# Query, key and value projections from seven products of quarters, with the biases in a weight row, in a graph attention and transformer kernel

## The chip, the cores and the metric

The kernel runs on one core of one Trainium2 chip. The metric is the device time of one execution in microseconds (us); lower is better. All inputs and outputs are float32, the adjacency int32.

## The reference

For 64 graphs of 256 nodes with 256 features, two layers follow each other. Layer 0 is two graph attentions, a residual with layer norm, and a feed-forward of 1024 with ReLU, again with residual and layer norm. Layer 1, where the change lies, is attention of 8 heads of 32, in which the values depend on the relation (0 to 3) that the adjacency gives, and a feed-forward of 1024 with GELU:

```python
q = (src @ Wq + bq).reshape(Bb, Nn, h, dh).transpose(0, 2, 1, 3)
k = (src @ Wk + bk).reshape(Bb, Nn, h, dh).transpose(0, 2, 1, 3)
scores = jnp.einsum('bhid,bhjd->bhij', q, k) / np.sqrt(dh)
attn = jax.nn.softmax(scores, axis=-1)
for r in range(Wv.shape[0]):
    v_r = (src @ Wv[r] + bv[r]).reshape(Bb, Nn, h, dh).transpose(0, 2, 1, 3)
    mask = (adj_matrix == r)[:, None]
    out = out + jnp.einsum('bhij,bhjd->bhid', attn * mask, v_r)
attn_out = out.transpose(0, 2, 1, 3).reshape(Bb, Nn, Dm) @ Wo + bo
x = _ln(src + attn_out, g1, beta1)
ff = jax.nn.gelu(x @ W1 + b1, approximate=False) @ W2 + b2
return _ln(x + ff, g2, beta2)
```

The adjacency that comes in holds only 0 and 1, so two of the four relations can occur.

## The kernel before, in words

Two paths are built. `narrow_path` computes everything under assumptions (adjacency of 0 and 1, sums of exponentials in range) and sums up checks of them; only where a check fails does `general_path` run after it. `checked` (L704) is the check of the adjacency: VectorE forms (a - 1) a and sums it per partition into a column of `other`; the sums are compared with 0 at L1448.

The graphs are taken in 32 groups of two. A group has T = 4 blocks of 128 nodes, 512 nodes in all. Features lie on partitions where they are contracted: `hT` holds 256 features as KB = 2 tiles of 128 partitions by 512 nodes. Group u goes through layer 0 one turn before it goes through layer 1, and its first graph attention one turn before that: `turn(y_, x_, z)` (L1155) works on three groups at once, y in layer 1, x in layer 0's feed-forward and z in the graph attentions. In turns 0 to 29 all three are there; turn 30 lacks z, turn 31 lacks x and z. On TensorE, SyncE, VectorE and ScalarE the order of instructions in these turns is the order of the Python code, up to small exchanges (`tc.manual_schedule`); in the last turn only TensorE and SyncE keep it.

The names that matter:

- `projection` (L979): q and k. Each is two output halves of 128 features; a half is two matmuls of 128x128 weights by 512 nodes into one bank of PSUM (L986), then a ScalarE activation adds the bias column and writes SBUF (L988).
- `values` (L992): for each of the 4 node blocks, two matmuls with 128 nodes as stationary operand and the 512 columns of `wv` (relation 0, and relation 1 minus relation 0) as moving one (L999); VectorE adds the bias row `rbv` (L1001).
- `weighted` (L1006): the scores of one graph and four heads (a "quad"), eight matmuls (L1015), and four exponentials on ScalarE (L1021). `masked` (L1024) multiplies by the adjacency (L1026), `node_sums` (L1029) adds over node blocks (L1031), `applied` (L1034) forms the products with the values (L1041) and the sums of the exponentials (L1044, tile `zo`), and `divided` (L1047) divides (L1052 to L1057). `add_blocks` (L780) then multiplies by `wo` (L786).
- `hidden_seven` (L842) and `HiddenOut` (L930): both feed-forwards already come from seven products of quarters. The quarters are halves of the features by the two graphs. VectorE makes four differences (L854), TensorE does seven products per half of the outputs (L871) into two banks, ScalarE copies one bank out (L880), VectorE adds the other to it (L883). Those banks are used again by later products, which therefore wait for the copy or the sum. In the second factor, VectorE makes the sums `eq` and `eaq` (L946), TensorE the products (L960), VectorE adds them to `y` (L968).
- `norm` (L805) computes means and variances on VectorE (L801, L802) and the reciprocal root on GpSimd (L812, L813); `applied_norm` (L818) makes `nm` on VectorE (L821) and applies it in four ScalarE activations (L828). `times` and `plus` (L836, L839) put the affine part on the residual, on VectorE.
- `normed_features` (L663) turns normed rows into features: VectorE transposes 32x32 blocks (L668), then 16 moves put them in place, 4 by GpSimd copies and 12 by SyncE transfers of 32 KB (L677, L687). With `natural` set, the result has nodes in order; this is the `hT` of layer 1.
- `folding` (L603) folds the layer norms' scale and shift into the next weights at the start, spread over the start of the program by `next(fold)`: `shifted` (matmuls with one column, L592), `scaled` on GpSimd (L599), `seven` and `seven_out` (the weight sums for the seven products, on GpSimd).
- The tiles of `work` are named by tags, two buffers each unless `bufs=1`; `bank` gives one of six banks of PSUM, and `po` and `zo` have one each.

The first lines of a turn are

```python
query(0)
query(1)
if X:
    applied_norm(X["y"], *X.pop("n"))
last = norm(waiting[0][0], 3, waiting[0][1]) if waiting else None
key(0)
key(1)
if X:
    X["hT"] = normed_features(x_, 0, X["y"])
    times(X["y"], rg1)
scores(0)
```

Of the kernel before, what the change touches and what calls it, by code (L numbers as in the profile page):

```python
# [9 lines left out]
F32 = mybir.dt.float32  # L10
# [6 lines left out]
P = 128  # L17
# [368 lines left out]
def narrow_path(  # L386
# [123 lines left out]
    def gat_weights():  # L510
# [5 lines left out]
        a1, a2 = columns([v.rearrange("f o -> (f o)") for v in (g_a1, g_a2)], "ga", nc.scalar, "k")  # L516
# [31 lines left out]
    lg1, lb1, bf1, lg2, lb2, bq, bk, lg3, lb3, b1 = columns(  # L548
        (g_g1, g_b1, g_bf1, g_g2, g_b2, t_bq, t_bk, t_g1, t_be1, t_b1), "cols", nc.scalar, "q")
    rg1, rb1, rg2, rb2 = row(g_g1, "rg1"), row(g_b1, "rb1"), row(g_g2, "rg2"), row(g_b2, "rb2")  # L550

    wq, wk, wo = weight(t_Wq, "wq"), weight(t_Wk, "wk"), weight(t_Wo, "wo")
# [4 lines left out]
    rbv = row(t_bv[0:2].rearrange("r f -> (r f)"), "rbv")  # L557
    nc.vector.tensor_tensor(wv[:, :, 1, :], wv[:, :, 1, :], wv[:, :, 0, :], ALU.subtract)
    nc.vector.tensor_tensor(rbv[:, F:], rbv[:, F:], rbv[:, :F], ALU.subtract)
# [3 lines left out]
    def seven(w, name):  # L563


        h = FF // 2
# [34 lines left out]
    wf1s, wf2s, w1s, w2s = [], [], [], []  # L601

    def folding():  # L603
# [8 lines left out]
        for w, bias, name in ((wq, bq, "bq"), (wk, bk, "bk")):  # L612
            shifted(w, range(KB), lb2, bias, name)
            scaled(w, lg2)
        yield
        ps = bank("rbvp")
        for k in range(KB):
            nc.tensor.matmul(ps, lb2[:, k:k + 1].to_broadcast([P, P]), wv[:, k].rearrange("p r f -> p (r f)"),
                             start=(k == 0), stop=(k == KB - 1))
        nc.vector.tensor_tensor(rbv, rbv, ps, ALU.add)  # L620
        scaled(wv.rearrange("p c r f -> p c (r f)"), lg2)
# [12 lines left out]
    for n, (rb, v) in enumerate(((rb1, g_bf2), (rb2, t_bo), (rb3, t_b2))):  # L634
        nc.gpsimd.tensor_add(rb, rb, row(v, None, rows[:, n, :F]))

# [25 lines left out]

    def normed_features(u, l, xn, natural=False, queues=(nc.sync,)):  # L663
# [7 lines left out]
        if natural:  # L671
            hT = work.tile([P, KB, TN], F32, tag="hT", name=f"hT{u}_{l}")
            to = hT.rearrange("c k (t a r) -> c (k t) a r", a=Q, r=32)
            for q in range(Q):
# [3 lines left out]
            return [hT[:, k] for k in range(KB)]  # L678
# [25 lines left out]
    def checked(u, aq):  # L704
        a = aq.rearrange("p t n -> p (t n)")
        nc.vector.scalar_tensor_tensor(a, a, 1.0, a, op0=ALU.subtract, op1=ALU.mult,
                                       accum_out=other[:, u:u + 1])
# [20 lines left out]
    class Softmax:  # L728

        def __init__(s, u, l, wh, rows, c):  # L730
            s.u, s.wh, s.rows, s.c = u, wh, rows, c
            s.s = (work.tile([P, T, N], F32, tag="s", name=f"s{u}_{l}", bufs=1) if u > 1 else
# [246 lines left out]
    def projection(u, hT, name, w, c):  # L979

        d = work.tile([P, KB, TN], F32, tag=name, name=f"{name}{u}", bufs=1)

        def step(m):
# [509 lines left out]
```

## Time and profile before

| | |
|---|---|
| median of 3 runs | 3075.3 us (3073.74, 3075.30, 3075.54) |
| span of the profiled execution, first to last instruction | 3072.8 us |
| what lies around the span, against the median | 2.5 us |
| mean granted TensorE clock | 0.995 |
| busy: TensorE, VectorE, ScalarE, GpSimd | 3031.3, 2595.7, 1602.2, 648.0 us |
| q and k products (L986, 512 records), values (L999, 512 records) | 232 and 228.5 us of TensorE |
| one full turn | 93.4 us |

The profile has no device time of its own for the profiled execution beside its span, so the median of the runs stands for it. A float32 matmul appears as two records; a few are missing from the trace, as can be seen from their counts. Times in the profile are in microseconds from the first instruction. In the chain of waits each line is a start, a length and the engine, tile and line that held the end up; in a timeline a line is a start, the busy time, the engine, the line, the operation with its tiles and shapes, and in brackets the idle time before it with what ended it.

### The profile page before, as it was taken

Reading aid. Unit: us, or ns where it says so; the run is one execution under the profiler, and the core shown is the slowest. Engines: PE = TensorE matmul, PEld = TensorE weight load, DVE = VectorE, ACT = ScalarE, POOL = GpSimd, SP = SyncE. Lnnn points to the kernel's source line nnn. Section 1 sums busy time; section 2 is a strip of 40 time slices with the busy share of each in tenths; the row PEclk is TensorE's granted clock in tenths of the full one; section 3 lists DMA queues with packets and bytes.
Section 4 is the critical chain, followed back from the end, with each engine's and each line's share of the span. In section 5 each row is a group of like instructions: output and inputs, shape, how many; then the busy total and the mean of one; then the engine's idle time right before and its main releaser. Section 6 shows DMA issues by size and latency. Waiting matters only on the chain.

```text
span 3072.8 us, 56424 instructions
## 1 busy us (share of the span) xinstructions
PE 3031.3 (99%) x21432; PEld 2330.1 (76%) x21432; DVE 2595.7 (84%) x4890; ACT 1602.2 (52%) x3212; POOL 648.0 (21%) x896
## 2 busy tenths in 40 slices
PE   7999999999999999999999999999999999999998
PEld 6677877778777778777787777787777787777866
DVE  4788888888888888888888888888888888888876
ACT  4455545555545555555555455555455554554553
POOL 3122121222211221212221112222112212122211
PEclk8999999999999999999999999999999999999999
DMA  5011111211111211112211112111112111121000
GB/s 149 13 37 35 34 39 25 44 41 35 35 35 32 44 37 32 39 26 43 44 33 35 40 25 44 37 36 35 30 38 44 35 34 39 25 44 37 18 13 16
DMA packets 427988, 113.37 MB, mean 37 GB/s; under 512 B 364568, under 2 KB 427072, under 8 KB 427712
## 3 DMA queue, kind: packets, MB, share of 16 engines
q1 hardware_dynamic: 417664, 102.46, 15.8%
q10 hardware_dynamic: 8992, 6.19, 0.8%
q8 instruction: 172, 2.82, 0.4%
q0 software_dynamic: 1056, 1.05, 0.1%
q14 instruction: 104, 0.85, 0.1%
HBM read 57.04 MB, written 16.78 MB: 24 GB/s over the span
## 4 chain that ended last, share of the span: by engine, by line
PE 90%; DVE 7%; DMA 1%; POOL 1%; ACT 1%; issue 0%; SPq 0%; ACTq 0%; POOLq 0%; DVEq 0%
PE yf L960 22%; PE h1a L871 15%; PE h1b L871 11%; PE po L1041 8%; PE vp L999 7%; PE sp L1015 4%; PE xpp L715 4%; PE yop L786 4%; PE qp L986 3%; PE kp L986 3%; PE ygp L786 3%; PE zo L1044 2%; PE hpp L775 2%; DVE s L750 2%; DVE yt L668 1%; DVE eaq L946 1%
## 5 line engine op out<-in xcount | busy, mean ns | idle before, releaser
L880 ACT COPY h<-h1b 128x512 f32<-128x512 f32 x384 | 224.6, 585 | 390.0 <-PE h1b L871 390.0
L828 ACT ACTIVATE y<-y,nm,rs 128x256 f32<-128x256 f32 x450 | 239.0, 591 | 238.4 <-DVE nm L821 234.1
L883 DVE TENSOR_TENSOR h<-h1a,h 128x512 f32<-128x512 f32 x384 | 263.6, 687 | 117.5 <-PE h1a L871 111.6
L1026 DVE TENSOR_TENSOR ea<-e,aT 128x1024 f32<-128x1024 f32 x256 | 309.5, 1239 | 54.3 <-ACT e L1021 54.3
L1021 ACT ACTIVATE e<-sp 128x512 f32<-128x512 f32 x512 | 264.3, 602 | 52.0 <-PE sp L1015 48.7
L1054 POOL TENSOR_TENSOR low<-low,rq 128x16 f32<-128x16 f32 x64 | 13.9, 218 | 1087.3 <-DVE rq L1053 1087.3
L685 POOL COPY hT<-yt 32x256 f32<-32x256 f32 x244 | 207.2, 849 | 59.0 <-DVE yt L668 51.4
L968 DVE TENSOR_TENSOR y<-yf,y 128x256 f32<-128x256 f32 x448 | 183.1, 409 | 39.7 <-PE yf L960 39.6
L999 PE MATMUL vp<-wv,hT 128*128 128x512 f32 x480 | 214.0, 599 | 0.0
L801 DVE BATCH_NORM_STATS2 st<-y 128x6 f32<-128x256 f32 x512 | 207.7, 408 | 5.5
L812 POOL TENSOR_SCALAR rs<-mv 128x4 f32<-128x4 f32 (+1 forms) x134 | 34.2, 255 | 720.7 <-DVE mv L802 454.6
L999 PEld LDWEIGHTS vp<-wv,hT 128*128 128x128 f32 x480 | 88.7, 190 | 110.4 <-issue 103.2
L840 DVE TENSOR_TENSOR y<-y,rb 128x1024 f32<-128x1024 f32 (+1 forms) x130 | 166.9, 1284 | 3.2
L988 ACT ACTIVATE q<-qp,cols 128x512 f32<-128x512 f32 x64 | 44.0, 687 | 238.3 <-PE qp L986 238.3
L914 ACT ACTIVATE h<-h,cols 128x512 f32<-128x512 f32 x256 | 167.0, 714 | 1.5 <-DVE h L883 1.1
L837 DVE TENSOR_TENSOR y<-y,rg 128x1024 f32<-128x1024 f32 (+1 forms) x130 | 161.8, 1245 | 2.2 <-ACT y L828 1.1
L1031 DVE TENSOR_TENSOR es<-e 128x1024 f32<-128x1024 f32 x128 | 155.5, 1215 | 0.0
L677 POOL COPY hT<-yt 32x256 f32<-32x256 f32 x120 | 115.6, 964 | 169.2 <-DVE yt L668 159.7
L1015 PEld LDWEIGHTS sp<-q,k 32*128 32x128 f32 x2048 | 92.5, 184 | 74.2 <-issue 44.8
L1015 PE MATMUL sp<-q,k 32*128 32x256 f32 x2048 | 146.6, 400 | 2.0 <-ACT k L988 2.0
L1041 PE MATMUL po<-e,v 128*32 128x256 f32 x2048 | 136.3, 384 | 0.0
L813 POOL TENSOR_TENSOR rs<-rs,mhalf 128x4 f32<-128x4 f32 (+1 forms) x134 | 134.5, 1004 | 8.2
(249 smaller groups left out, 7191.4 us busy)
## 6 DMA issues: line engine op xcount, KB each, us to landing
hT<-yt SPq DMA_DIRECT2D x912, 32.0 KB, 2.0
y<-in_x_dram SPq DMA_DIRECT2D x32, 512.0 KB, 4.7
xq<-in_x_dram SPq DMA_DIRECT2D x240, 64.0 KB, 2.2
aq<-in_adj_dram SPq DMA_DIRECT2D x240, 64.0 KB, 2.4
out_dram<-y SPq DMA_DIRECT2D x30, 512.0 KB, 2.9
hT<-yt ACTq DMA_DIRECT2D x180, 32.0 KB, 1.9
wf<-in_L_gnn_w_ff_dram SPq DMA_DIRECT2D x2, 1024.0 KB, 8.1
w<-in_L_gnn_W_dram SPq DMA_DIRECT2D x2, 1024.0 KB
```

Source lines behind the costliest of these rows:

```text
L786: nc.tensor.matmul(ps[:, i * F:(i + 1) * F], lhs(t, k), rhs(b, k), start=(k == 0), stop=(k == n - 1))
L801: nc.vector.bn_stats(st[:, t, :], y[:, t, :])
L828: mark["normed"] = nc.scalar.activation(y[:, t, :], y[:, t, :], AF.Identity, bias=nm[:, t:t + 1], scale=rs[:, t:t + 1])
L871: nc.tensor.matmul(ps[:, i * N:(i + 1) * N], w_[:, f * P:(f + 1) * P], m, start=first and i == 0, stop=True, skip_group_check=True)
L880: mark["copied"] = nc.scalar.copy(out(h, o, b), pair(ps))
L883: mark["added"] = nc.vector.tensor_tensor(out(h, o, b), pair(one[h]), out(h, o, b), ALU.add)
L960: nc.tensor.matmul(s.ps[n][:, i * F2:(i + 1) * F2], a[:, k, i * P:(i + 1) * P], w_[:, k, :], start=n in (1, 2, 5) and i == 0 and k == 0, s ...
L999: nc.tensor.matmul(ps, hT[k][:, t * P:(t + 1) * P], wvf[:, k, :], start=(k == 0), stop=(k == KB - 1))
L1015: nc.tensor.matmul(ps[a][:, j * N:(j + 1) * N], k_[hp, m, j0:j0 + P], q[hp, m, b * N:(b + 1) * N], start=True, stop=True)
L1021: mark[f"exp{b * KB + m}"] = nc.scalar.activation(e[:, a, :], ps[a], AF.Exp, scale=isd)
L1026: nc.vector.tensor_tensor(ea[:, a:a + 2, :], e[:, a:a + 2, :], ab[:, None, :].to_broadcast([P, 2, NB * N]), ALU.mult)
L1041: nc.tensor.matmul(po[hp, m * N:(m + 1) * N], vs[:, hp], w[:, a, j * N:(j + 1) * N], start=(n == 0), stop=(n == len(terms) - 1))
```

## The change

1. The weights of q and k are laid into one tile `wqk` (256 by 512; each half of the columns holds 128 outputs of q and then the same 128 of k), and each of `wqk` and `wv` gets the weight sums of the seven products through `seven`. A class `Projections` takes the place of `projection` and `values`: four differences on VectorE into a tile of tag `e` (`sums`), then seven products for q and k together and seven for the values, two matmuls of 256 columns each. Products 2, 5 and 3 go through one bank, 1, 6, 7 and 4 through another; for the values these are the banks `zo` and `po`. ScalarE copies four results out of each pair of banks, VectorE adds three.
2. The biases go into a weight row. A normed row sums to zero, so feature 224 is minus the sum of the others: `joined` subtracts its weights from all rows and puts the bias in its row, and `with_ones` writes ones over that feature in `hT` (a GpSimd memset of one partition). The scalings of q, k and v weights move from GpSimd to VectorE, and the shifts of all three are matmuls of 512 columns.
3. In the turn, products of q and v alternate, the scores of the first quad stand among them, with their exponentials and masks in two parts; the norm of x is applied in two parts; the second quad's scores follow all the products. `times` on x's residual moves from before the first scores to just before `plus`.
4. `checked` is a ScalarE activation (a - 0.5) squared, summed, and compared with 0.25 for each entry; in a turn it stands after the second graph attention's exponentials, and the loads of the next adjacency follow it there.
5. Tags: the graph attention's scores of groups 2 and up share `v`, `rz` goes to `es`, and `qk` holds what `q` and `k` held.

```diff
+    def joined(w, name, bias):
+        ps, pr = bank(f"{name}bp"), bank(f"{name}rp")
+        for k in range(KB):
+            nc.tensor.matmul(ps, lb2[:, k:k + 1].to_broadcast([P, P]), w[:, k],
+                             start=(k == 0), stop=(k == KB - 1))
+        only = work.tile([P, 1], F32, tag="ve", name=f"{name}o")
+        nc.vector.tensor_mul(only, ident[:, one], lg2[:, KB - 1:KB])
+        nc.tensor.matmul(pr, only.to_broadcast([P, P]), w[:, KB - 1], start=True, stop=True)
+        nc.vector.tensor_tensor(bias, bias, ps[one].rearrange("p (o f) -> p o f", o=2), ALU.add)
+        for k in range(KB):
+            nc.vector.scalar_tensor_tensor(w[:, k], w[:, k], lg2[:, k:k + 1], pr,
+                                           op0=ALU.mult, op1=ALU.subtract)
+        nc.vector.tensor_copy(w[one, KB - 1].rearrange("p (o f) -> p o f", o=2), bias)
...
-        for w, bias, name in ((wq, bq, "bq"), (wk, bk, "bk")):
-            shifted(w, range(KB), lb2, bias, name)
-            scaled(w, lg2)
+        joined(wqk, "wqk", brow[:, 0:2])
+        wqks.extend(seven(wqk, "wqk"))
         yield
...
-        scaled(wv.rearrange("p c r f -> p c (r f)"), lg2)
+        joined(wvf, "wv", brow[:, 2:4])
+        wvs.extend(seven(wvf, "wv"))
...
+    def with_ones(hT):
+        nc.gpsimd.memset(hT[KB - 1][one], 1.0)
+        return hT
...
-            for q in range(Q):
+            for q in reversed(range(Q)):
...
-            return [hT[:, k] for k in range(KB)]
+            return with_ones([hT[:, k] for k in range(KB)])
...
     def checked(u, aq):
         a = aq.rearrange("p t n -> p (t n)")
-        nc.vector.scalar_tensor_tensor(a, a, 1.0, a, op0=ALU.subtract, op1=ALU.mult,
-                                       accum_out=other[:, u:u + 1])
+        nc.scalar.activation(a, a, AF.Square, bias=mhalf[:, 0:1], accum_out=other[:, u:u + 1])
...
+        def step(s, x, n):
+            a11, a12, a22, s1, s2, s3, s4 = wqks if x == "q" else wvs
+            w, m = {1: (a11, s.h[0][0]), 2: (a12, s.h[1][0]), 5: (s1, s.t[0]), 3: (s4, s.h[1][1]),
+                    6: (s2, s.t[1]), 7: (s3, s.t[2]), 4: (a22, s.t[3])}[n]
+            if n == 1:
+                s.one[x] = s.bank(x, 1)
+            elif n == 2:
+                s.two[x] = s.bank(x, 0)
+            ps = (s.two if n in (2, 5, 3) else s.one)[x]
+            for i in range(2):
+                l, r = (w[:, i * P:(i + 1) * P], m) if x == "q" else (m[:, i * P:(i + 1) * P], w)
+                nc.tensor.matmul(ps[:, i * N:(i + 1) * N], l, r, start=n in (1, 2, 5) and i == 0, stop=True,
+                                 skip_group_check=True)
+            if n == 2:
+                s.copied(x, 0, 0, ps)
+                s.added(x, 0, 0)
+            elif n == 5:
+                s.copied(x, 1, 1, ps)
+            elif n == 3:
+                s.copied(x, 0, 1, ps)
+            elif n == 6:
+                s.added(x, 0, 1)
+            elif n == 7:
+                s.added(x, 1, 1)
+            elif n == 4:
+                s.copied(x, 1, 0, ps)
...
         with order:
-            query(0)
-            query(1)
+            p.sums()
+            p("q1 v1 q2")
             if X:
-                applied_norm(X["y"], *X.pop("n"))
+                applied_norm(X["y"], *X["n"], [0, 1])
             last = norm(waiting[0][0], 3, waiting[0][1]) if waiting else None
-            key(0)
-            key(1)
+            p("v2 q5")
             if X:
+                applied_norm(X["y"], *X.pop("n"), [2, 3])
                 X["hT"] = normed_features(x_, 0, X["y"])
-                times(X["y"], rg1)
-            scores(0)
+            scores(0, ())
+            p("v5")
+            powers(0, (0, 1))
...
+            p("q3 v3")
+            masks(0, (0,))
+            powers(0, (2, 3))
             if waiting:
                 applied_norm(waiting[0][1], *last)
-            if X:
-                v = values(y_, hT, range(T // 2, T), v)
+            p("q6 v6 q7 v7")
+            masks(0, (2,))
+            totals(0)
+            p("q4 v4")
...
             first("4a 7b rb")
             if X:
+                times(X["y"], rg1)
                 plus(X["y"], rb1)
...
             Z["m"].exp(1)
+            checked(z, Z["aq"])
+            if z + 1 < NG:
+                load_adjacency(z + 1)
...
-            checked(z, Z["aq"])
-            if z + 1 < NG:
-                load_adjacency(z + 1)
...
-    nc.vector.tensor_scalar(good[:, 1:2], c[:, 3:4], 0.0, None, op0=ALU.is_le)
+    nc.vector.tensor_scalar(good[:, 1:2], c[:, 3:4], 0.25 * NG * T * N, None, op0=ALU.is_le)
```

## The prediction

> **What bounds the kernel now.** I read the shares of the engines first, then the chain of waits for the whole span and for one turn of the loop over groups, then the timelines of VectorE and ScalarE in that turn, last SyncE's queue.
>
> ```profile
> PE 3031.3 (99%) x21432; PEld 2330.1 (76%) x21432; DVE 2595.7 (84%) x4890; ACT 1602.2 (52%) x3212; POOL 648.0 (21%) x896
> ...
> PE 90%; DVE 7%; DMA 1%; POOL 1%; ACT 1%; issue 0%; SPq 0%; ACTq 0%; POOLq 0%; DVEq 0%
> ```
>
> TensorE is never out of work, and 90% of the chain is its own. VectorE, at 84%, is close behind. The chain in order of time (start, length, what), one turn's first stage and a piece of its hidden layer:
>
> ```profile
> 1604.16 3.44 PE qp L986 x8
> 1607.60 3.43 PE kp L986 x8
> 1611.03 1.08 PE sp L1015 x16
> 1612.11 7.06 PE vp L999 x16
> 1619.17 1.08 PE sp L1015 x16
> 1620.25 1.86 PE po L1041 x32
> ...
> 1631.57 0.86 PE h1a L871 x4
> 1632.43 0.94 PE h1b L871 x4
> ```
>
> The stage runs from 1604.16 to 1620.25: **16.09 us**, of which q, k and values take 3.44 + 3.43 + 7.06 = **13.93**, without a gap. The next turn's qp begins at 1697.60, so a turn is 93.4 us. L871 is already a product of seven: two 128x128 by 256 matmuls, each two records, in 0.86 us.
>
> Timelines of the same turn (start, busy, engine, line; in brackets the idle time before and what ended it), ScalarE, then VectorE:
>
> ```profile
> 1608.22 2.06 ACT L828 ACTIVATE y<-y,nm,rs 128x256 f32<-128x256 f32 x4
> ...
> 1633.41 0.59 ACT L880 COPY h<-h1b 128x512 f32<-128x512 f32 x1 [1.22 <-PE h1b L871]
> ```
> ```profile
> 1606.84 0.16 DVE L821 SCALAR_TENSOR_TENSOR nm<-mv,rs 128x4 f32<-128x4 f32 x1 [1.24 <-POOL rs L813]
> ...
> 1609.36 1.43 DVE L668 STREAM_TRANSPOSE yt<-y 128x256 f32<-128x256 f32 x4 [0.22 <-ACT y L828]
> ...
> 1628.85 0.72 DVE L1052 STREAM_TRANSPOSE rz<-zo 128x512 f32<-128x512 f32 x1 [2.36 <-PE zo L1044]
> ...
> 1636.15 0.69 DVE L883 TENSOR_TENSOR h<-h1a,h 128x512 f32<-128x512 f32 x1 [0.77 <-PE h1a L871]
> ```
>
> VectorE waits little: 2.36 us at L1052 and 0.77 at L883 are its two reserves in the first half of a turn. And the twelve moves of the next group's features, whose landing VectorE (L854) and TensorE wait for (two turns):
>
> ```profile
> 1797.79 7.54 SPq L687 DMA_DIRECT2D hT<-yt  x12
> ```
> ```profile
> 2732.92 8.58 SPq L687 DMA_DIRECT2D hT<-yt  x12
> ```
>
> **What the Trainium skill says.** "TensorE: Matmul & The Clock Gate", section "Back-to-back issue gap": the spacing of a stream of matmuls goes with their columns, and weight loads run beside them. The trace agrees in proportion: 512 columns take 3.44/8 = 0.43 us a record, 256 columns 0.86/4 = 0.215; halving costs nothing. "PSUM — Partial Sum Buffer", section "PSUM bank collisions raise a hardware error": accesses of different engines to a bank must be kept apart by waits. So a product written into a bank waits for the copy out of it, as L871 does here (0.94 in place of 0.86). The same page, "Engine vs sequencer instructions": ScalarE and VectorE are strict queues; the timelines show nothing out of order. "ScalarE: Activation LUTs", section "What ACT_TABLE_LOAD costs": an ACTIVATE takes 0.28 us + 0.833 ns an element; exp on 512 measures 0.602, nearer its 0.186 for constant scale and bias.
>
> **The change, part by part.** One profiled span is 3072.8 us; the median of the three runs, 3075.3, is 2.5 above it. I carry differences over to the median.
>
> *Products.* Removed: 13.93 us a turn. Added: 14 products x 0.86 = 12.04. If all ran without a gap: 1.89 a turn, 60 us over 32 turns. But where 16 full-bank matmuls needed no answer from another engine, 14 products now share four banks, and each re-use waits for a ScalarE copy or a VectorE sum. Prices: a copy starts 0.20 after its product's end (the product at 1633.21, the copy at 1633.41) and takes 0.59; a sum starts 0.27 after (1635.88, 1636.15) and takes 0.69; a product that waited ends about 1.03 after its release (0.96 to 1.12 where L871 waited for L883). I walk through the stage in the order in which the built program has each queue, zero at the first product:
>
> - q1, v1, q2, v2 end at 0.86, 1.73, 2.59, 3.45. Copy of q2: 2.79 to 3.38. So q5 ends at 4.41 (0.10 lost). VectorE's sum for q: 3.41 to 4.10. The first scores follow: 5.49.
> - On VectorE `nm` of group x now stands behind that sum: 4.26 (it was 2.8). ScalarE's two norms wait for it, and the copy of v2 stands behind them: 4.30 + 2 x 0.515 + 0.59 = 5.92. So v5 ends at 6.95, not 6.35: 0.60 lost. q3: 7.81.
> - The copy of v5 stands behind the other two norms: 7.35 to 7.94; v3 ends at 8.97 (0.30 lost). q6 9.83, v6 10.69.
> - VectorE's first mask (1.14) can't start before the exps, 8.98; the sum of q6 follows at 10.2 to 10.89; q7 ends at 11.92 (0.37 lost), v7 12.78.
> - Sum of q7 12.19 to 12.88, q4 13.91 (0.27 lost), v4 14.77; the copy of q4 ends at 14.70, and the second scores at 15.9.
>
> So **15.9 against 16.09: 0.2 gained a turn, 1.7 of 1.9 given back in waits**. The uncertainty is that of five waits, 0.07 each, and of the norms' place, 0.2: from -0.3 to +0.7 a turn. 30 full turns: **-6.0**.
>
> *VectorE.* Added: 6 sums x 0.687, 4 subtractions x 0.421; gone: 4 value additions x 0.680, the check 1.216: +1.9 us a turn. The subtractions take the check's place before the turn (1.1 against 1.14 back to back), so nothing is late at zero. The transposes of x end at 8.45 in place of 6.6; SyncE's twelve moves (7.54 to issue, and at most 1.35 to land, since L854 ran at 1619.82 unhindered) then arrive at 17.5, not 15.7. VectorE idles from 15.95 to 17.5 where it had none, and comes to L1052 at 24.2; zo is there at 24.4. TensorE wants the features at 18.1. Both covers hold by 0.2 to 0.6 us. In eight of 27 turns the moves took 8.0 to 8.6: there about 0.25 is lost, **+2**.
>
> *`times` later.* 1.25 us goes from VectorE at 6.7 to before L840 (34.5). It uses up idle time of 0.41, 0.25 and 0.32 behind it; the shares are ready at 45.2, and L786 wants them at 45.6. At nothing; without that cover 0.5 a turn.
>
> *Check on ScalarE.* In place of 1.22 us of VectorE, one ACTIVATE on 1024 elements: 0.28 + 0.85 = 1.1 (estimate from the ScalarE page), inside ScalarE's wait of 3.86 us for z: nothing. The eight adjacency loads that follow it on SyncE now start some 6 us earlier, right behind the feature moves and far ahead of the next ones. No table load is added.
>
> *The row of ones.* GpSimd's memset waits for three moves, which are now issued first; it ends some 10 us ahead of q2, and only a sum for lowg (0.2) is queued behind it. Nothing (0 to 0.2 where the first turn waits for it).
>
> *Start and end.* At the start GpSimd's two scalings of wv (0.70 + 0.69) no longer stand before L812 on the chain, two checks leave VectorE, while TensorE gets 4 more 512-column matmuls and VectorE four scalings: **-1.5**, bounds -3 and +3. At the end the last turn has idle ScalarE and VectorE and keeps about half of 1.9, while `times` may cost turn 30 half a microsecond: **-1**.
>
> Sum: -6 + 2 - 1.5 - 1 = -6.5, rounded with the part of the gain that the last two turns may keep: **3068**.
>
> **The rivals.** *Most waits hidden*: the norms don't stand in the way, or releases are shorter, so that half of the 1.7 comes back: 0.9 x 32 + 1.5 = 30, 3045. For it: the order alternates q and v, so that one product always covers. Against it: 0.20 + 0.59 and 0.27 + 0.69 are themselves as long as a product, and TensorE's gain must be met by VectorE, which has 1.9 more to do. *Features late* (slower): if the transposes end 0.6 us later than I have, the landing passes 18.1, TensorE waits at the first hidden product and VectorE carries the delay past its reserves; from there each further 0.5 us costs 0.5 a turn: 0.5 x 30 = 15, 3090. For it: the landings were limiting in 22 places already, 19.1 us in all. Against it: every step before 8.45 has a slack known to about 0.2. *Nothing moves*: what TensorE gains is lost where it waits for VectorE's `eaq` (L946, 0.5 a turn): 3076. For it: VectorE's busy time. Against it: VectorE meets TensorE again at L968 just before, with 0.48 idle. *The check fails*: were ScalarE's square of a half not exactly a quarter, the sum would pass its limit and the general path would run after all, for thousands of microseconds; nothing in the profile speaks for it, and I give it 0.02.
>
> **How the numbers follow.** About 0.2% (6.2 us) is what can be told from no change. Forecast 0.43 (own range 3058 to 3078; six in ten below 3069.2), most waits hidden 0.22, nothing moves 0.13, features late 0.20, check 0.02. Faster: 0.26 + 0.22 = 0.48; same: 0.17 + 0.12 = 0.29; slower 0.23. The range 3044 to 3086 cuts the outer halves of the two outer rivals.
>
> **What would show it.** Right: first scores' end to second scores' end as walked, L1051 products (changed kernel) with waits on ScalarE's copies (v5, v3) and VectorE's sums (q7, q4) of some 1.5 us a turn; stage 15.9. Wrong: a stage under 15.3 or over 16.4; long waits of the hidden products for `hT`; the start longer than before; `nm` at its old place.

## The result, and the profile after

The changed kernel takes **3071.55 us** (median of 12 runs, 3069.44 to 3072.67) against 3074.7 (12 runs, 3073.05 to 3077.15) on the same chip: ratio **0.9989**, 95% interval 0.9981 to 0.9997. That is 3.2 us less, inside the band of 0.2%. The profiled executions have spans of 3067.8 and 3072.8, both at a clock of 0.995. The profiled execution of after is the quickest of its twelve, so that the 5.0 us between the spans flatter the change a little.

From the page of after, the busy line and the shares of the chain:

```profile
PE 3003.6 (98%) x22192; PEld 2460.3 (80%) x22192; DVE 2624.0 (86%) x5025; ACT 1684.2 (55%) x3404; POOL 678.4 (22%) x930
...
PE 85%; DVE 9%; ACT 2%; issue 2%; DMA 1%; SPq 1%; POOL 1%; DVEq 0%; POOLq 0%; ACTq 0%
```

TensorE is busy for 28 us less, but only 85% of the chain is its own (90 before): most of what it was spared it spends waiting. The chain of waits of after shows where, in one turn (start, length, what):

```profile
1600.40 0.86 PE qk L1051 x4
1601.26 0.86 PE v L1051 x4
1602.13 0.88 PE qk L1051 x4
...
1604.25 0.17 DVE nm L846
...
1604.95 0.59 ACT y L853
1605.54 0.48 ACT v L1034
1606.01 0.04 issue
1606.06 1.13 PE v L1051 x4
1607.19 0.86 PE qk L1051 x4
1608.05 1.08 PE v L1051 x4
...
1610.11 0.35 DVE nm L846
1610.46 0.61 DVE qk L1038
1611.07 0.04 issue
1611.12 1.13 PE qk L1051 x4
1612.25 0.86 PE v L1051 x4
1613.11 1.05 PE qk L1051 x4
1614.16 0.86 PE v L1051 x4
1615.03 1.08 PE sp L1082 x16
1616.10 1.86 PE po L1110 x32
1617.97 0.43 PE zo L1113 x8
1618.40 1.24 issue
1619.64 1.10 PE h1b L896 x4
```

The stage now runs from 1600.40 to 1616.10: **15.70** us against 16.09. Fourteen products at 0.86 and two scores at 1.08 would be 14.20, so 1.5 us a turn are waits: the copy of v2 (L1034) stands behind a norm (L853) that stands behind `nm` (L846), and the product after it, v5, is released at 1606.01; q7 is released by VectorE's sum (L1038) at 1611.07. Products that show 1.05 to 1.13 in place of 0.86 have waited. At 1618.40 TensorE stands 1.24 us, and the profile names no releaser; its next product reads the next group's features, and VectorE's first difference of these begins at the same moment (1619.62), so I take it that they have not landed before. The view of waits of after names them (who waited for whom, total us, times, longest; PEld is TensorE's weight load, which waits for the product's bank):

```profile
DVE tt L879 <- DMA hT<-yt: 71.0, 42, 3.6
PEld qk L1051 <- DVE qk L1038: 33.2, 64, 2.3
PEld v L1051 <- ACT v L1034: 29.5, 63, 0.7
PEld yf L985 <- DVE eaq L971: 15.0, 30, 0.5
DVE rz L1121 <- PE zo L1113: 8.2, 18, 1.5
```

Before, VectorE waited 19.1 us for the features (71.0 now), and 70.1 us for `zo` ahead of its first transposition of the shares (8.2 now): the two changed by about as much (51.9 more, 61.9 less), which I read as its reserve having gone into waiting for features. The wait for `eaq` is what it was, 15.0 in 30 turns.

Where the 5.0 us between the two spans come from, from the starts of q1 and of the scores in each turn. In this table and below the stage is taken from the timelines, which put the start of q1 0.16 ahead of the chain: 16.25 before, 15.86 after.

| | before | after | difference |
|---|---|---|---|
| first instruction to the first q1 | 104.31 | 102.81 | -1.5 (102.8 to 104.6 in the kernels below, e7 left out, which moves work out of the start) |
| turn 0 | 97.31 | 98.02 | +0.7 |
| turns 1 to 29: stage, mean of each | 16.25 | 15.88 | -0.375 x 29 = -10.9 |
| turns 1 to 29: lateness of the first hidden product against the usual turn, sum | 0 | 5.0, in 8 turns | +5.0 |
| turns 1 to 29: the rest, sum of what exceeds the usual | 1.5 | 1.3 | -0.2 |
| turn 30 | 73.82 | 74.06 | +0.2 |
| turn 31, and to the last instruction | 86.10 | 87.77 | +1.7 |

### The profile page after: what moved, and what is told of

It is laid out like the page before. It is cut to its first block, busy times and chain, and to the rows that moved or that the text cites. A ratio compares the mean times of both kernels' runs of the same rounds, so it can differ in the third digit from the quotient of the medians.

```text
span 3067.8 us, 58503 instructions
## 1 busy us (share of the span) xinstructions
PE 3003.6 (98%) x22192; PEld 2460.3 (80%) x22192; DVE 2624.0 (86%) x5025; ACT 1684.2 (55%) x3404; POOL 678.4 (22%) x930
## 3 DMA queue, kind: packets, MB, share of 16 engines
q0 software_dynamic: 1056, 1.05, 0.1%
## 4 chain that ended last, share of the span: by engine, by line
PE 85%; DVE 9%; ACT 2%; issue 2%; DMA 1%; SPq 1%; POOL 1%; DVEq 0%; POOLq 0%; ACTq 0%
PE yf L985 22%; PE h1a L896 15%; PE h1b L896 11%; PE po L1110 7%; PE qk L1051 5%; PE v L1051 5%; PE xpp L740 4%; PE yop L811 4%; PE ygp L811 3%; PE sp L1082 3%; PE hpp L800 2%; PE zo L1113 2%; DVE s L775 2%; DVE yt L694 1%; DVE eaq L971 1%
## 5 line engine op out<-in xcount | busy, mean ns | idle before, releaser
L853 ACT ACTIVATE y<-y,nm,rs 128x256 f32<-128x256 f32 x450 | 243.8, 607 | 140.1 <-DVE nm L846 135.8
L1034 ACT COPY qk<-qk 128x512 f32<-128x512 f32 x128 | 75.3, 589 | 286.9 <-PE qk L1051 286.9
L838 POOL TENSOR_TENSOR rs<-rs,mhalf 128x4 f32<-128x4 f32 (+1 forms) x134 | 146.6, 1094 | 8.4
L1082 PE MATMUL sp<-qk 32*128 32x256 f32 x2048 | 146.6, 400 | 0.1
L742 ACT COPY xp<-xpp 128x260 f32<-128x260 f32 x128 | 45.4, 386 | 171.5 <-PE xpp L740 171.4
L1038 DVE TENSOR_TENSOR qk<-qk,qk 128x512 f32<-128x512 f32 x96 | 65.9, 686 | 83.9 <-ACT qk L1034 65.1
L896 PE MATMUL h1a<-tt,wf 128*128 128x256 f32 x512 | 134.2, 386 | 0.3 <-DVE h L908 0.3
```

The lines of the kernel that those rows point to most:

```text
L853: mark["normed"] = nc.scalar.activation(y[:, t, :], y[:, t, :], AF.Identity, bias=nm[:, t:t + 1], scale=rs[:, t:t + 1])
L896: nc.tensor.matmul(ps[:, i * N:(i + 1) * N], w_[:, f * P:(f + 1) * P], m, start=first and i == 0, stop=True, skip_group_check=True)
L1082: nc.tensor.matmul(ps[a][:, j * N:(j + 1) * N], k_[hp, m, j0:j0 + P], q[hp, m, b * N:(b + 1) * N], start=True, stop=True)
```

## The experiments

**Theory**: TensorE is held at two places that are tied to each other, in products that wait for copies and sums, and at the features, which are wanted earlier the faster the stage gets. **Rival A**: ScalarE's copies behind the norms are all there is to it. **Rival B**: VectorE's total work sets the pace. A third view, that a product saved is simply time saved, is tried last. Ratios are against the kernel before, run beside it on the same chip; "features late" is the lateness of the first hidden product, as in the table above, from one profile of each kernel.

| | us | ratio, 95% interval | stage, usual | features late, sum (turns) |
|---|---|---|---|---|
| changed kernel | 3071.55 | 0.9989 (0.9981 to 0.9997) | 15.86 | 5.0 (8) |
| e1_shift_first | 3066.04 | 0.9971 (0.9960 to 0.9982) | 15.64 | 7.7 (12) |
| e2_stats_first | 3066.35 | 0.9974 (0.9963 to 0.9984) | 15.87 | 2.0 (5) |
| e3_both | 3053.49 | 0.9931 (0.9917 to 0.9944) | 15.48 | 0 |
| e4_ones_vector | 3072.66 | 0.9993 (0.9984 to 1.0001) | 15.87 | 5.4 (10) |
| e5_exp_split | 3046.53 | 0.9910 (0.9896 to 0.9923) | 15.21 | 1.2 (5) |
| e6_check_vector | 3070.04 | 0.9987 (0.9980 to 0.9994) | 15.87 | 5.7 (8) |
| e7_scaling_later | 3071.40 | 0.9990 (0.9983 to 0.9996) | 15.87 | 5.8 (9) |
| e8_last_turn | 3085.38 | 1.0037 (1.0023 to 1.0050) | 15.87 | 5.1 (9) |
| e9_qk_alone | 3076.70 | 1.0009 (1.0002 to 1.0015) | 16.17 | 0 |
| e10_ends | 3048.55 | 0.9914 (0.9900 to 0.9927) | 15.21 | 1.6 (5) |
| e11_times_back | 3090.80 | 1.0053 (1.0039 to 1.0067) | 16.72 | 0.5 (2) |
| e12_qk_covered | 3050.28 | 0.9921 (0.9907 to 0.9935) | 15.43 | 0 |

### The two waits, apart and together

e1_shift_first (`norm_shift` is the part of `applied_norm` that makes `nm`, and `made` leaves it out there):

```diff
-            p("q1 v1 q2")
+            p("q1 v1")
+            if X:
+                norm_shift(*X["n"])
+            p("q2")
             if X:
-                applied_norm(X["y"], *X["n"], [0, 1])
+                applied_norm(X["y"], *X["n"], [0, 1], made=True)
```

> Edit: on VectorE, nm of group x is made ahead of the sum for q instead of behind it; nothing else moves. Theory (the gain of TensorE is lost at two places: in products that wait for ScalarE's copies behind the norms, and in features of the next group that come late): v5 no longer waits, v3 waits less, the stage from q1 to the second scores shortens from 15.86 us by about 0.45 to 15.4. But the transposes stay where VectorE's own queue has them, so the features are wanted 0.45 earlier and don't come earlier: the pause ahead of the first hidden product grows by 0.2 to 0.3 a turn. Net -0.2 a turn, about -6: 3065 to 3066. Rival A (the copies behind the norms are all there is to it): the whole 0.45 stays, -13: 3058. Rival B (VectorE's total work sets the pace): 0, 3071.

e2_stats_first:

```diff
+            if waiting:
+                early_mv = moments(waiting[0][0], 3, waiting[0][1], range(NB))
             p("q1 v1 q2")
...
-            last = norm(waiting[0][0], 3, waiting[0][1]) if waiting else None
+            last = norm(waiting[0][0], 3, waiting[0][1], mv=early_mv) if waiting else None
```

> Edit: half of the statistics for the last norm of the group that is done (two of four blocks, 1.16 us of VectorE) are made in VectorE's pause of 2.1 us ahead of the sum for q, instead of between nm and the transposes. Theory: the stage stays at 15.86; the transposes end about 0.6 us earlier, SyncE's moves begin at 7.65 after q1 instead of 8.24, VectorE's wait for them falls from 2.07 to 1.5 a turn on average, and most of the 5.0 us that TensorE loses ahead of the first hidden product goes: about -3.5, 3068. Rival A (copies behind the norms alone): 0, 3071.5. Rival B (VectorE's total work): 0.

e3_both has both diffs.

> Both edits of e1_shift_first and e2_stats_first. Theory: the two losses are tied to each other, so both together give more than the sum of each: stage 15.4, moves begin near 6.8 after q1, no late features: -0.45 x 30 and -5 = -18.5, 3053. Rival A: as e1 alone, 3058. Rival B (VectorE's total work): 3068 to 3071.

The times were 3066.0, 3066.35 and 3053.5. Against the changed kernel's 3071.55, the first edit brings 5.5, the second 5.2, both 18.1, where the sum of each would be 10.7. In the profiles, turns 1 to 29 became 4.0, 4.0 and 17.5 us shorter. The table shows the one half of the reason: e1 alone shortens the stage and pays for it in late features (7.7 in place of 5.0), e2 alone mends most of the features (2.0 are left) and leaves the stage. The other half is that e1 alone shortens the stage by 0.22 and both together by 0.38. Rivals A (3058, 3071.5, 3058) and B (3071, 3071.5, 3068 or more) miss all three. The timeline of VectorE in one turn of e1_shift_first (start, busy, engine, line, instruction; in brackets the idle time before it and what ended it), the first mask and the first difference of features:

```profile
1515.19 1.39 DVE L1095 TENSOR_TENSOR ea<-e,aT 128x1024 f32<-128x1024 f32 x1 [0.21 <-ACT e L1091]
...
1524.35 0.43 DVE L879 TENSOR_TENSOR tt<-hT 128x256 f32<-128x256 f32 x1 [1.86 <-DMA hT<-yt]
```

and in the same turn of e3_both (q1 starts at 1506.84 there and at 1499.12 here):

```profile
1507.46 1.22 DVE L1095 TENSOR_TENSOR ea<-e,aT 128x1024 f32<-128x1024 f32 x1 [1.26 <-ACT e L1091]
...
1515.58 0.42 DVE L879 TENSOR_TENSOR tt<-hT 128x256 f32<-128x256 f32 x1 [0.97 <-DMA hT<-yt]
```

VectorE begins on the features 17.51 us after q1 in the first, 16.46 in the second. e1's time is the expected one by luck, since both of its terms came out at about half: late features cost 2.7 us more where 6 to 9 were expected, and the stage gained 0.22 where 0.45 was expected. The reason for the second is the mask, which takes 1.39 in place of 1.22; the sum that q7 waits for stands behind it. GpSimd's copies of the features run beside the mask in both kernels. What differs is how long the copy that is already running when the mask begins still has to run. The timelines of GpSimd at that place, of e1_shift_first and of e3_both:

```profile
1515.10 0.39 POOL L711 COPY hT<-yt 32x256 f32<-32x256 f32 x1 [0.49 <-DVE yt L694]
```
```profile
1507.18 0.39 POOL L711 COPY hT<-yt 32x256 f32<-32x256 f32 x1
```

In e1 the copy ends 0.30 after the mask's start, in e3 0.12 after it. The mask's length follows this remainder through the kernels of the study: 1.22 where the remainder is 0.12 or there is none (e3, the changed kernel), 1.25 at 0.17 (e5), 1.32 at 0.24 (e9), 1.39 at 0.30 (e1), 1.42 at 0.33 (e11), 1.44 at 0.37 (the kernel before). From 0.17 on, the mask ends 1.08 us after the copy. (The pair of engines comes up again under e10_ends.) So the theory, which tied the two edits together by the features alone, covers about half of what both bring beyond the sum of each, 4.7 us of 9.4 in these turns; the stage brings 4.5, since e2's edit, by making the copies earlier, also frees the mask.

e5_exp_split follows the same thread one wait further:

```diff
-            scores(0, ())
+            scores(0, (0,))
             p("v5")
-            powers(0, (0, 1))
+            powers(0, (1,))
```

> Edit: e3_both, and on ScalarE the first exponential of the first scores goes ahead of the copy of v5 instead of behind it (the second stays behind). In e3_both ScalarE idles 0.42 there, VectorE waits until 8.34 for both exponentials, then the mask (1.22) stands ahead of the sum for q6, for which q7 waits until 10.50, while v6 ends near 10.1. Theory (every microsecond that releases a waited product earlier is gained as long as the features hold): the mask starts near 7.85, the sum for q6 is free to start when q6 is done, q7 starts 0.35 earlier, stage 15.13 instead of 15.48, turn 92.33: -10.5 against e3_both, 3043. Rival (TensorE is by now held elsewhere in the turn, at VectorE's eaq or at the features): 3053.

The time was 3046.5, another 7.0 us less, of the 10.5 expected. q7 in the timeline of TensorE, in e3_both and in e5_exp_split:

```profile
1509.61 1.13 PE L1051 MATMUL qk<-tq,wqk 128*128 128x256 f32 x4 [0.26 <-DVE qk L1038]
```
```profile
1505.64 1.13 PE L1051 MATMUL qk<-tq,wqk 128*128 128x256 f32 x4
```

That is 10.49 and 10.22 after q1; the pause ahead of it is gone. The stage is 15.21 (15.13 expected), and 1.2 us of late features are back, as the stage again outruns them. This is the quickest kernel of the study, 28 us below the kernel before (interval 24 to 32 from the ratio).

### Single parts of the change undone

e6_check_vector puts the check back, and with it the adjacency loads, to their old place:

```diff
-        nc.scalar.activation(a, a, AF.Square, bias=mhalf[:, 0:1], accum_out=other[:, u:u + 1])
+        nc.vector.scalar_tensor_tensor(a, a, 1.0, a, op0=ALU.subtract, op1=ALU.mult, accum_out=other[:, u:u + 1])
```

> Edit: the changed kernel with the check of the adjacency back on VectorE, at its old place, and the adjacency loads behind it again. VectorE gets 1.22 us a turn more, ahead of the last norm statistics before q1. The prediction's step: nothing, since VectorE then eats into its pause of 2.1 us ahead of the sum for q, and nm stands behind that sum anyway: 3070 to 3073. Rival B (VectorE's total work sets the pace): 1.2 a turn, +36, 3107.

The time was 3070.0: 1.22 us a turn more on VectorE cost nothing (the intervals of the two ratios overlap), and the stage is unchanged to 0.01. Rival B is out by 37 us. VectorE, busy for 86% of the span, is not the bound; what counts is where an instruction stands.

e11_times_back shows that from the other side:

```diff
                 X["hT"] = normed_features(x_, 0, X["y"])
+                times(X["y"], rg1)
...
-                times(X["y"], rg1)
                 plus(X["y"], rb1)
```

> Edit: the changed kernel with times of group x back at its old place, right behind the transposes. The prediction's step called the move free; the reverse need not be. Theory: VectorE has 0.51 us of pause there, so the first mask comes 0.55 later, with it the sum for q6, q7 and the second scores: stage 16.4; the features are wanted that much later, so their 5.0 us go: +0.55 x 30 - 5 = +11.5, 3083. Rival (VectorE's place has no weight): 3071.

The time was 3090.8, more than expected: the stage is 16.72 in place of 16.4. The timeline of VectorE in one turn of it:

```profile
1523.47 1.41 DVE L694 STREAM_TRANSPOSE yt<-y 128x256 f32<-128x256 f32 x4
1524.92 1.23 DVE L862 TENSOR_TENSOR y<-y,rg 128x1024 f32<-128x1024 f32 x1
1526.07 1.42 DVE L1095 TENSOR_TENSOR ea<-e,aT 128x1024 f32<-128x1024 f32 x1
```

Some 1.2 us of VectorE's time, which cost nothing at the check's place, cost 0.86 a turn here, ahead of the mask and the sum that q7 waits for; the mask begins while a GpSimd copy still has 0.33 to run, and takes 1.42. Without this move the change would have been slower than the kernel before.

### The start and the end

e4_ones_vector, e7_scaling_later and e10_ends are about turn 0. The timelines of TensorE and GpSimd of the changed kernel there:

```profile
108.27 1.68 PE L1051 MATMUL qk<-h2T,wqk 128*128 128x256 f32 x4 [3.48 <-POOL h2T L686]
109.74 1.91 PE L1051 MATMUL v<-wv,h2T 128*128 128x256 f32 x4
```
```profile
102.84 4.47 POOL L603 TENSOR_SCALAR w<-w,cols 128x1024 f32<-128x1024 f32 x2 [3.77 <-PE b1sp L596]
107.39 0.25 POOL L837 TENSOR_SCALAR rs<-mv 128x4 f32<-128x4 f32 x1
107.70 0.52 POOL L686 MEMSET h2T<- 1x512 f32 x1
```

These products show 1.68 and 1.91 us where the same product shows 1.03 in a later turn: from 108.2 to 111.7 TensorE's granted clock is 0.57. e4_ones_vector:

```diff
-        g[0]["hT"] = with_ones(to_features(g[0]["y"], "h2T0"))
+        g[0]["hT"] = with_ones(to_features(g[0]["y"], "h2T0"), nc.vector)
```

> Edit: in the first turn the row of ones is written by VectorE instead of GpSimd, where it stood behind 4.47 us of scaling of w1. Theory: TensorE's 3.5 us of waiting for it in turn 0 go, but the next waits are near (the subtractions behind two long VectorE instructions, and the power for the norm, which stays behind the same scaling on GpSimd): -2.4, bounds -1 and -3.5, 3069. If the first turn's loss is hidden by the other waits: 0.

e7_scaling_later:

```diff
-        next(fold)
         for u in range(NG):
...
             sums(0)
+            if y_ == 0:
+                next(fold)
```

> Edit: the changed kernel with the last part of the folding (GpSimd's 4.47 us of scaling of w1, and what follows from it) moved from ahead of the first turn to behind the first sums of that turn, so that neither the row of ones nor the power for the norm stands behind it on GpSimd. e4_ones_vector took only the row of ones away and found the next wait, that of the copy of v2 for nm, in its place. Theory: with both away the first turn loses some 4 us less: 3067 to 3068. If yet another wait is behind: 3071.

In e7_scaling_later the call that moves holds the last part of the folding, small matmuls and then the scaling of w1. Neither gained anything. e4 (3072.7) took the wait for the row away, and v5 then waited 1.75 for the copy of v2, which hangs on the norm whose power stands behind the same scaling: turn 0's stage was 21.5, longer than the 20.8 of the changed kernel. The timeline of TensorE in e4, v5:

```profile
114.90 1.82 PE L1051 MATMUL v<-wvs,tq 128*128 128x256 f32 x4 [1.75 <-ACT v L1034]
```

TensorE's waits in turn 0 fell only from 3.6 to 2.9 us, and more products run slowly: 16 records of products in place of 7 start some 0.43 apart instead of 0.215, with a granted clock of 0.54 from 104.6 to 108 and 0.53 from 114.9 to 118.5. e7 (3071.4) did shorten the stage, from 20.8 to 17.2, and no product of the projections is slow there. But the small matmuls, some 1.8 us, now stand in turn 0 instead of the start, and they hold a bank until VectorE reads it; the third scores waited 1.71 for that. Turn 0 took 100.2 in all, and start and turn 0 together 201.6 against 200.8.

e8_last_turn:

```diff
-                                            ("PE", "SP", "DVE", "Activation")[:4 if X else 2]})
+                                            ("PE", "SP", "DVE", "Activation")[:4 if X else 3]})
```

> Edit: the changed kernel with VectorE's queue in the order of the code in the last turn too. There the products of the projections wait 3.7 us in all for sums on VectorE that stand behind four long instructions of another part (1.21 each) and two masks. Theory: the last turn gets 1.5 to 2.5 us shorter, 3069.5. Rival: the order of the code is worse later in that turn, 0 or longer.

The timeline of VectorE of the changed kernel in the last turn, with q7 waiting 1.87 us for the sum at 2992.22:

```profile
2988.81 1.23 DVE L971 TENSOR_TENSOR sq_aq<-h,wq 128x1024 f32<-128x1024 f32 x1
2989.95 2.35 DVE L1095 TENSOR_TENSOR ea<-e,aT 128x1024 f32<-128x1024 f32 x2
2992.22 0.68 DVE L1038 TENSOR_TENSOR qk<-qk,qk 128x512 f32<-128x512 f32 x1
```

(Of the 3.7 in the expectation, 2.2 are waits for such sums; 1.2 is a wait for the features ahead of q1, 0.3 one for a copy.) In e8 the stage of that turn fell from 18.3 to 16.1, as the theory had it; then the four long sums and everything after them stood in line on VectorE, and the turn took 101.9 in place of 87.8. That is the rival's case, and the time was 3085.4.

e10_ends takes the two faults apart (`mark["projected"]` is the sum of a projection, `mark["moved"]` GpSimd's copy of features, `behind` queues behind it):

```diff
         shifted(w1, range(FB // 2, FB), lb3, b1, "b1")
+        yield
         scaled(w1, lg3)
...
             sums(0)
+            if y_ == 0:
+                with behind("moved"):
+                    next(fold)
...
                 for _ in range(ends):
-                    piece()
+                    with behind("projected"):
+                        piece()
```

> Edit: e5_exp_split, and two edits at the ends: in the first turn GpSimd's scaling of w1 is queued behind the moves of the next group's features (its matmuls stay where they were, which e7_scaling_later did not do), and in the last turn VectorE's four long sums of the other part are queued behind the last sum of a projection (the rest of that queue stays as it was, which e8_last_turn did not do). Theory: turn 0 gets 3.5 us shorter and keeps it, the last turn 1 to 2 us: 3046.5 - 5 = 3041.5. Rival (the ends have other waits close behind): 3046.

The time was 3048.55, no better than e5 (the intervals of the two ratios overlap). The last turn is 2.5 us shorter than in e5 (86.30, 88.84). Of that, 1.4 is q7's wait, which fell from 1.86 to 0.49. The rest comes with TensorE's clock: after that wait, products of e5 are slow, as this line of its timeline shows, and the granted clock from 2969 to 2972 is 0.66:

```profile
2970.27 1.91 PE L1051 MATMUL v<-wv,tq 128*128 128x256 f32 x4
```

Nine kernels of the study, the changed one among them, have no edit aimed at the last turn. Six of their profiles have such slow products there, and the turn takes 88.7 to 89.0; three, the changed kernel's among them, have none, and it takes 87.6 to 87.9. So the +1.7 of the last turn in the first table is the smaller of two sizes, and e10's edit is worth 1.5 or 2.5.

Turn 0 gained 3.6 in its stage and lost 7.2 behind it. The timelines of VectorE and GpSimd of e10_ends there (line numbers one higher than in the changed kernel):

```profile
122.10 1.50 DVE L880 TENSOR_TENSOR tt<-hT 128x256 f32<-128x256 f32 x1
123.63 1.38 DVE L880 TENSOR_TENSOR tt<-hT,tt 128x256 f32<-128x256 f32 x1
```
```profile
117.61 1.26 POOL L585 TENSOR_TENSOR w2t<-w 128x512 f32<-128x512 f32 x1
118.84 2.25 POOL L573 TENSOR_TENSOR w1s<-w 128x512 f32<-128x512 f32 x1
121.04 2.27 POOL L586 TENSOR_TENSOR w2t<-w,w2t 128x512 f32<-128x512 f32 x1
123.27 1.45 POOL L574 TENSOR_TENSOR w1s<-w1s,w 128x512 f32<-128x512 f32 x1
```

The subtractions that take 0.42 elsewhere take 1.38 to 1.50 beside GpSimd, and GpSimd's own sums 1.45 to 2.27 in place of 1.26. The Trainium skill, "SBUF — State Buffer", section "Who interferes with whom", says that a VectorE instruction with two inputs in SBUF contends with a GpSimd instruction that reads SBUF, and calls the ports that they share an exclusive lock. These rows agree, and they show the delay on both sides in turn: the first subtraction ends 0.28 us after the GpSimd sum that was running when it began, the GpSimd sum that began at 123.27 ends 1.1 after the first subtraction, the second subtraction 0.28 after that sum, and so on. The masks of 1.25 to 1.44 above fit the same reading: a mask that begins during a copy is held until the copy ends. No run took GpSimd's copies away by themselves. Behind the subtractions, TensorE waits 2.05 and 1.58 us for two masks, and its granted clock from 126 to 136 is 0.76.

### q and k alone

```diff
-            p("q1 v1 q2")
+            p("q1 q2 V0")
...
-            p("v2 q5")
+            p("q5")
...
-            p("v5")
+            p("V1")
...
-            p("q3 v3")
+            p("q3")
...
-            p("q6 v6 q7 v7")
+            p("q6 V2")
+            p.kept(2, nc.vector.tensor_copy)
+            p("q7 V3")
...
-            p("q4 v4")
+            p("q4")
```

`V0` to `V3` are the plain products of the values, one block of nodes each; `kept` is the copy out of the bank.

> Edit: the changed kernel with the seven products for q and k alone; the values come from four full-bank products of two matmuls each as before (bias in the weight row, so that their sums on VectorE become copies: three on ScalarE, one on VectorE), put between the products of q as cover: q1 q2 V0 q5, scores, V1 q3 q6 V2 q7 V3 q4. TensorE has 0.86 us a turn more to do than with all in seven. Theory (the waits, not the number of products, set the stage): every waited product of q has 1.73 us of values or scores between it and its release, so that nothing waits; the stage is 12.94 + 2 x 1.08 and small gaps = 15.2 to 15.4 instead of 15.86. The sum for q is done 0.85 earlier and nm right behind it, the transposes end near 7.2 instead of 8.2, so that the late features (5.0 us) go too: -0.55 x 30 - 5 = -21, 3050. Rival (a product less is time less): the values' 0.86 a turn comes back, +26, 3097; in between if the waits go in part.

The time was 3076.7, not the 3050 expected. The features were never late, as expected, and no product of q waited. But the last product was now q4, and its copy lay bare ahead of the second scores. The timeline of TensorE in one turn of e9_qk_alone (its line numbers are 2 to 10 off the changed kernel's):

```profile
1524.04 1.03 PE L1053 MATMUL qk<-tq,wqk 128*128 128x256 f32 x4
1525.74 1.15 PE L1092 MATMUL sp<-qk 32*128 32x256 f32 x16 [0.68 <-ACT qk L1036]
```

e12_qk_covered mends that order (its diff is against e9_qk_alone; the copies move with their products, and the last turn's edit of e10_ends comes with it):

```diff
-            p("V1")
             powers(0, (0, 1))
...
-            p("q3")
+            p("q3 q6 V1")
...
-            p("q6 V2")
-            p.kept(2, nc.vector.tensor_copy)
-            p("q7 V3")
+            p("q7 V2")
+            p.kept(2, nc.vector.tensor_copy)
...
-            p("q4")
+            p("q4 V3")
```

> Edit: e9_qk_alone with the values put where a product of q waits or where the scores wait: q1 q2 V0 q5, scores, q3 q6 V1 q7 V2 q4 V3; the sum for q6 goes ahead of the first mask on VectorE; and the last turn's edit of e10_ends (worth 1.5 to 2.5). In e9_qk_alone nothing waited until q4, but q4 was last, and its copy (0.21 after its end, 0.58 long) stood bare ahead of the second scores, 0.85 us; a full-bank product between q5 and q3 covered a wait that the scores cover anyway. Theory: stage 15.2 to 15.4, no late features, turns of 92.4 to 92.6: 3045 to 3050, level with e5_exp_split, though TensorE has 26 us more to do than there. Rival (a product less is time less, e9's order was not at fault): no better than 3072.

The time was 3050.3, at the upper end of what was expected; the stage is 15.43, the turns 92.6. With 0.86 us a turn more for TensorE it comes within 3.8 us of e5_exp_split (whose interval of the ratio overlaps with this one, and which lacks its edit of the last turn, 1.5 or 2.5), and lies 21 us below the change that has seven products for the values too. So a product saved is not time saved: as the change orders them, the seven products of the values do not earn their place against a version without them whose waits are covered; with waits mended on both sides, as far as these two kernels mend them, they are worth 0.2 us in a usual turn (92.40 against 92.61). Each of the two still has waits (some 0.9 and 0.2 us in its stage, against the sum of its products and scores), so this is no last word on what the seven could be worth.

## Why the prediction was right, and where its sizes were off

The time came out 3.6 us above the predicted 3068, inside the range and inside the forecast's own range. It is a change within 0.2%, to which I had given 0.29; I had given 0.48 to a larger gain. The mechanism was the one predicted: TensorE gains 1.89 a turn and gives 1.5 of it back in waits of its own making. That the total came so near is in part luck, since the errors of the terms cancel: in the profiles the products gained 4.9 us more than forecast, while the features cost 3.0, the start 0.7 and the end 2.9 more. By the steps:

- *Products and their waits*: right in place, small in size. v5, v3, q7 and q4 were the late ones, as walked; the second scores ended at 15.70 instead of 15.9. v5 ended 0.16 earlier than walked and v3 0.24. I had put ScalarE's instructions end to end at their full length, 0.59; in the timeline they start 0.47 to 0.49 apart. The Trainium skill, "ScalarE: Activation LUTs", in the section that the prediction drew on ("What ACT_TABLE_LOAD costs"), says that such instructions overlap by about 93 ns back to back, which agrees; I did not use it. The term was -0.2 a turn and measured -0.37.
- *VectorE, features*: right in mechanism, short in size: +2 was put down, +5.0 measured. Two assumptions failed. "At most 1.35 to land" was read in one turn of the kernel before, where VectorE came to the features without waiting; in other turns of the same profile it waited, and its differences begin up to 2.1 us after SyncE's last issue has ended, which was there to be read. Now, in the turns that begin at 1412.6 and 1600.2, the differences begin 3.3 and 3.5 us after SyncE's last issue has ended. The second assumption was that only turns with long issues lose: the wait for features falls in turns whose issues take their usual 7.5 as well as in long ones. The rival *features late* was thus partly real: in 8 of 29 turns, TensorE paused for 0.1 to 1.4, which I had named as a sign of being wrong. e2 and e3 show it by taking it away in part and in full. The 1.9 a turn more of VectorE's work, which this step began with, measured 0.7 (busy for 81.64 of a turn, 80.97 before): I had added full lengths, but of instructions back to back the sums start 0.60 apart and the subtractions 0.34; the rest of the difference I have not traced.
- *`times` later* at nothing: right for the new place, but it hid a term. e11 prices the old place at 19 us in the changed kernel; the move is what keeps the change from a loss.
- *Check on ScalarE* at nothing: right (e6).
- *The row of ones*, 0 to 0.2: wrong as a reading. I had looked at the later turns, where it is early; in turn 0 it stands behind 4.5 us of scaling, and TensorE waits 3.5 for it. Taking that wait away gained nothing, since other waits and slow products lie behind it (e4, e7, e10).
- *Start*: -1.5 was forecast, and -1.5 and +0.7 measured, for the start and for turn 0; but the start itself moves by as much (102.8 to 104.6) between profiles of kernels that share it. *End*: -1 forecast, +1.9 measured. I had counted on idle engines in the last turn; its VectorE queue is not in the order of the code, and sums of projections stood behind four long instructions. e10's last turn is 1.5 us shorter than that of the changed kernel's profile.
- *Most waits hidden* did not happen; but e5 shows that a good part of the waits can be hidden by order alone, and reaches 3046.5, near the 3045 of that rival. *Nothing moves*: no, the wait for `eaq` stayed at 15.0 while e3 and e5 passed their gains on in full.

## What to carry to other kernels

When a full-bank product is split into smaller ones that share banks, count the releases, not only the cycles: each re-use here needed another product or two of cover (a copy takes 0.59, a sum 0.69, a product 0.86), also ahead of whatever reads the last one, and the engine that releases must have nothing waiting in front. A stage that gets faster wants its next inputs earlier by the same amount; edits to the one and to the other should be tried together, since here each alone gave 5 us and both gave 18 (half of the surplus was a mask that no longer began during a GpSimd copy). And before an instruction is moved off a busy engine, ask where it stands: 1.2 us a turn on VectorE was worth nothing at one place and 19 us at another.

## What was not expected of the hardware

VectorE's subtraction of two SBUF operands went from 0.42 to 1.38 to 1.50 us beside GpSimd's sums, which themselves went from 1.26 to 1.45 to 2.27. Each was held until the other's instruction ended, and a move off the path at the start cost more than it saved. A mask paid nothing for a copy that ended within 0.12 us of its start, and 0.17 for one that ended 0.30 after it. TensorE's granted clock was 0.53 to 0.57 in stretches of some 3.5 us in the first turn, where products show 1.7 to 1.9 us in place of 1.03. In the last turn, six of nine profiles show such products after a wait of some 1.9 us (0.66 for 3 us in e5), and three show none; what decides it stays open. The landing of the same twelve transfers, issued in the same 7.5 us, differs by some 2 us from turn to turn; what decides that was not settled.
